# GpSimd's share of the products of delta u and B in a selective scan: one-tensor multiplies by a scalar of the partition, 20 of 64

## The chip, the cores and the metric

The kernel runs on one core of a Trainium2 chip. The metric is the device time of one execution in microseconds (us), as the median of the runs. A trace comes from one more execution, taken by the hardware profiler.

The engines are named as in the profile: PE is TensorE's matmuls and PEld its weight loads, DVE is VectorE, ACT is ScalarE, POOL is GpSimd, SP is SyncE. L1580 is line 1580 of the kernel.

## The reference, cut to what matters

Four layers follow one another on an image of 2 x 128 x 128 pixels with 128 channels: window attention, a Fourier layer, a recurrent convolution, and a selective scan over four orders of the pixels. Only the selective scan is touched. For each direction k it computes, over a sequence of L pixels, with 256 channels d and 16 states n:

```python
delta = softplus(delta + delta_bias)
def step(h, inp):
    ut, dt, bt, ct = inp
    dA = jnp.exp(dt[..., None] * A4)
    h = dA * h + (dt * ut)[..., None] * bt[:, :, None, :]
    y = jnp.einsum('bkdn,bkn->bkd', h, ct)
    return (h, y)
```

The term `(dt * ut)[..., None] * bt` is the product that the change is about: for each pixel, 256 channels of delta u times 16 values of B.

## The kernel before, in words

`layer3_scan` (L1245 onwards) cuts the work into 256 **parts**: 2 images x 4 directions x 32 stretches of 512 pixels. A part has 8 **slots**. Slot s holds 4 tiles of 128 rows (4 states x 32 channels) by 512 pixels; with `q, e = divmod(s, 2)`, q is the group of four states and e the half of the channels. All slots of all parts are numbered on, 2048 in all, and the loop at L1649 walks through them with a fixed lead or lag for each step:

- `exponentials(g + 1)` (L1554): four ACT instructions write `da`, the decay of each pixel (L1561), one slot ahead.
- `kept(g - 1)` (L1631): one small ACT copy saves the last state of the slot before (L1637). It waits for that slot's scans.
- `products(g + 2)` (L1566): the products of delta u and B, two slots ahead, into a buffer `but` (five of them). Here the rows are 128 pixels, and `bt[:, tb, c]` holds one value of B for each pixel. A slot makes 2 blocks of pixels (`j`) x 4 states (`n`) = 8 products of 128 x 256, so a part makes 64. Slot `2q` makes pixel blocks tb = 0 and 1 of the state group q, slot `2q + 1` makes tb = 2 and 3. Some go to POOL (L1580), the others to ACT (L1585).
- `weighted(g - 1)` (L1639): one POOL multiply of 128 x 2048 by C, in place (L1643).
- `tiles(g)` (L1604): for each of the four tiles PE turns four blocks of `but` into a PSUM tile `ups` (L1617, three buffers), and DVE runs the recurrence over it (L1625). A tile needs all four pixel blocks, so both slots of `products` of its state group.
- `sums(g - 2)` (L1589): PE sums the weighted states into `yps` (L1599).

In between, steps of the parts to come and of those done are placed by a written table (L1534): `projected` (ACT, L1358) at the head of slot 7, `softplus_a` (ACT, L1392 and L1393) at the head of slot 1, `softplus_c` (ACT, L1405) in the middle of slot 2, and some small DVE work among the scans (L1399, L1413, L1420, L1429, L1466, L1488, L1493).

`in_order` (L114) ties each engine to the order in which the program was written. So each engine runs its instructions one after the other as the loop emits them, and an engine that waits holds back everything that it has behind.

The buffers around the change are `but` (five), `hs` and `da` (three each), `du` and `bt` (two each). POOL issues no DMA in this stage, and SP's queue carries the loads and stores.

Before the change, POOL takes state `n == 3`, except pixel block 3 in the even groups q. That is 2 of a slot's 8 products in slots 0, 2, 3, 4, 6 and 7, and 1 in slots 1 and 5: 14 in a part. ACT makes the other 50.

Of the kernel before, what the change touches and what calls it, by code (L numbers as in the profile page):

```python
# [11 lines left out]
ALU = mybir.AluOpType  # L12
# [3 lines left out]
P = 128  # L16
# [1228 lines left out]
def layer3_scan(tc, cs, ins, xs, xst, yc, ys):  # L1245
# [11 lines left out]
    nc = tc.nc  # L1257
    NS, DR, NX, T = 16, 8, 40, 512
    with ExitStack() as ctx:
# [52 lines left out]
        def tag_of(i):  # L1312
            return "_".join(map(str, parts[i]))
# [252 lines left out]
        def products(g):  # L1566

            i, s = divmod(g, 8)
            q, half = divmod(s, 2)
            v = held[i]  # L1570
            but = five.tile([P, 2, 8, 4, 32], F32, name=f"but_{tag_of(i)}_{s}", tag="but")
            v[("but", q, half)] = but
            bt = v["bt"]
            du = v["du"].rearrange("p t (g c) -> p t g c", c=32)
            for j in range(2):
                tb = 2 * half + j
                for n in range(4):
                    c = DR + 4 * q + n
                    if n == 3 and (tb < 3 or q % 2):
                        nc.gpsimd.tensor_tensor(  # L1580
                            but[:, j, :, n, :], du[:, tb],
                            bt[:, tb, c : c + 1].unsqueeze(2).to_broadcast([P, 8, 32]), ALU.mult,
                        )
                    else:
                        nc.scalar.activation(  # L1585
                            but[:, j, :, n, :], du[:, tb], AF.Copy, scale=bt[:, tb, c : c + 1]
                        )
# [60 lines left out]
        with in_order(tc):  # L1648
            for g in range(-15, slots + 7):  # L1649
                at(g, "head")  # L1650
                if 0 <= g + 1 < slots:
                    exponentials(g + 1)
                if 0 <= g - 1 < slots:
                    kept(g - 1)
                at(g, "mid")
                if 0 <= g + 2 < slots:
                    products(g + 2)
                if 0 <= g - 1 < slots:
                    weighted(g - 1)
                if 0 <= g < slots:  # L1660
                    tiles(g)
                else:
                    for j in range(4):
                        at(g, j)
                if 0 <= g - 2 < slots:
                    sums(g - 2)
                at(g, "end")
# [230 lines left out]
```

## Time and profile before

| | us |
|---|---|
| runs shown: median of 3 (lowest to highest) | 18375.93 (18361.79 to 18383.79) |
| profiled execution, first to last instruction (span) | 18336.7 |
| DVE busy | 15970.0 (87%) |
| ACT busy | 14905.8 (81%) |
| PE busy | 14346.5 (78%) |
| POOL busy | 11817.0 (64%) |

The profiled execution has only its span in the records; the median of the runs is 39.2 us above that span. The shares in the table are means over four layers that differ much. The line of 40 slices, each 1/40 of the span, shows where the engines are busy (a digit is the busy share in tenths):

```profile
DVE  6776666336999899999999999999999999999996
ACT  4665666334546799999999999999999999999984
POOL 0000000011000599999999999999999999999981
```

POOL's digits rise to 9 in the 15th slice, at about 14/40 x 18337 = 6418 us, and stay there up to the 39th. This is the scan stage. Everything ahead of it (three layers and the convolution of the fourth) and the short stage behind it are not touched.

### The profile page before, as it was taken

To read this page: it belongs to the slowest core of one execution; us is meant where nothing else is said; L and a number is where in the kernel's file an instruction comes from. 1 tells how busy PE (TensorE), PEld (TensorE's weight loads), DVE (VectorE), ACT (ScalarE), POOL (GpSimd) and SP (SyncE) were. 2 spreads that over 40 slices of the span, in tenths; PEclk is the share of its full clock that TensorE was granted. 3 is DMA by queue.
4 is the path that set the end of the run, shared out by engine and by line. 5 is a ranking of instruction groups with operands and counts; after the bars stand their busy time and mean duration, and the time that the engine had idled before them with its cause. 6 is when DMAs were issued, how large, how long until landed. Compare 5 with 4: busy or idle time off the path is not lost. (4 is left out here: it accounts for less than half of the span.)

```text
span 18336.7 us, 277675 instructions
## 1 busy us (share of the span) xinstructions
PE 14346.5 (78%) x97794; PEld 8284.5 (45%) x97794; DVE 15970.0 (87%) x20729; ACT 14905.8 (81%) x30049; POOL 11817.0 (64%) x6490
## 2 busy tenths in 40 slices
PE   7888888887668677777777777777777777777778
PEld 5555555664223344444444444444444444444445
DVE  6776666336999899999999999999999999999996
ACT  4665666334546799999999999999999999999984
POOL 0000000011000599999999999999999999999981
PEclk9999999889889899999999999999999999999989
DMA  2000000121115544444444455544444444445546
GB/s 45 23 24 23 17 18 16 61 65 56 56 51 191 155 116 116 121 127 127 125 116 116 118 127 129 128 121 115 116 125 128 129 125 117 116 119 127 127 131 192
DMA packets 1232638, 1859.32 MB, mean 101 GB/s; under 512 B 124877, under 2 KB 591565, under 8 KB 1228942
## 3 DMA queue, kind: packets, MB, share of 16 engines
q1 hardware_dynamic: 1157374, 1817.40, 37.6%
q10 hardware_dynamic: 73872, 24.16, 0.5%
q8 instruction: 776, 12.71, 0.3%
q14 instruction: 616, 5.05, 0.1%
HBM read 1396.64 MB, written 444.60 MB: 100 GB/s over the span
## 5 line engine op out<-in xcount | busy, mean ns | idle before, releaser
L1625 DVE TENSOR_TENSOR_SCAN hs<-da,states,ups 128x512 f32<-128x512 f32 x8192 | 9931.7, 1265 | 255.4 <-PE ups L1617 238.7
L1643 POOL TENSOR_TENSOR hs<-hs,cb 128x2048 f32<-128x2048 f32 x2048 | 9399.9, 4590 | 318.0 <-POOL but L1580 198.6
L1617 PE MATMUL ups<-ident,but 128*128 128x128 f32 x32768 | 5560.5, 301 | 2617.4 <-DVE hs L1625 1715.1
L1617 PEld LDWEIGHTS ups<-ident,but 128*128 128x128 f32 x32768 | 3859.2, 150 | 6207.6 <-DVE hs L1625 3515.8
L1585 ACT ACTIVATE but<-du,bt 128x256 f32<-128x256 f32 x12800 | 5350.7, 500 | 4.5 <-DVE du L1466 4.2
L1561 ACT ACTIVATE da<-db,na 128x512 f32<-128x512 f32 x8192 | 5238.6, 713 | 18.6 <-DMA db<-dd 15.8
L1599 PE MATMUL yps<-hs,sel 128*32 128x512 f32 x16384 | 2482.5, 682 | 50.4 <-POOL hs L1643 44.3
L1580 POOL TENSOR_TENSOR but<-du,bt 128x256 f32<-128x256 f32 x3584 | 2148.5, 619 | 17.0 <-DVE du L1466 17.0
L306 POOL TENSOR_TENSOR xres<-xres,rowb 128x256 f32<-128x256 f32 x128 | 94.3, 737 | 2440.3 <-DMA xres<-in_x 1744.7
L391 ACT COPY pT<-tps 128x512 f32<-128x512 f32 x1280 | 723.6, 585 | 1104.3 <-PE tps L386 1104.1
L386 PE MATMUL tps<-ident,s 128*128 128x128 f32 x8192 | 1223.7, 286 | 437.4 <-DVE pT L389 271.0
L358 DVE CUSTOM_DVE_ANT_1 s<-sps,relbias 128x512 f32<-128x512 f32 x2048 | 1321.7, 683 | 133.2 <-PE sps L341 127.9
L386 PEld LDWEIGHTS tps<-ident,s 128*128 128x128 f32 x8192 | 896.4, 143 | 1029.4 <-issue 498.5
L371 ACT ACTIVATE s<-s,nm 128x1024 f32<-128x1024 f32 x1024 | 1166.2, 1141 | 126.8 <-DVE nm L369 124.1
L1156 POOL MEMSET xpad<- 128x34 f32 x8 | 1.3, 162 | 1170.1 <-PE xs L1030 1105.8
L341 PE MATMUL sps<-kc,qT 32*128 32x512 f32 x4096 | 614.7, 668 | 1.9 <-DVE qT L326 1.2
L1637 ACT COPY states<-hs 128x4 f32<-128x4 f32 x2048 | 384.4, 188 | 247.5 <-DVE hs L1625 247.5
L389 DVE COPY pT<-tps 128x512 f32<-128x512 f32 x768 | 528.1, 688 | 55.9 <-PE tps L386 53.2
L1599 PEld LDWEIGHTS yps<-hs,sel 128*32 128x32 f32 x16384 | 339.4, 114 | 476.1 <-issue 301.9
L1349 PE MATMUL xdps<-xc,xpw 128*40 128x512 f32 x1024 | 540.8, 610 | 12.4 <-POOL xd L1286 12.4
L734 POOL TENSOR_TENSOR xr<-xr,row_ln_b 128x512 f32<-128x512 f32 x64 | 81.2, 1271 | 708.2 <-DMA xr<-x 474.7
L1381 PE MATMUL dtps<-xd,dtw 65*128 65x512 f32 x1024 | 534.0, 603 | 0.0
(287 smaller groups left out, 16171.3 us busy)
## 6 DMA issues: line engine op xcount, KB each, us to landing
db<-dd SPq DMA_DIRECT2D x1024, 512.0 KB
cb<-cd SPq DMA_DIRECT2D x1024, 256.0 KB
xc<-xs SPq DMA_DIRECT2D x256, 512.0 KB
dd<-dl SPq DMA_DIRECT2D x256, 512.0 KB
ut<-xst SPq DMA_DIRECT2D x128, 512.0 KB
yc<-ysb SPq DMA_DIRECT2D x128, 512.0 KB
yf<-yc SPq DMA_DIRECT2D x128, 512.0 KB
ys<-yt SPq DMA_DIRECT2D x128, 512.0 KB
```

What stands on the lines that cost most here:

```text
L341: nc.tensor.matmul(sps, v["qT"][hp, qt * P : (qt + 1) * P], kc[b, wh + g][hp, ww : ww + 2].rearrange("p a r c -> p (a r c)"), start=True, ...
L358: nc.vector.tensor_tensor_reduce(blocks(v["s", qt][:, h, 512 * g : 512 * g + 512]), blocks(v["sps", qt, g][h]), bias[:, h, :, r0 : r0 + WS ...
L371: nc.scalar.activation(s[:, h, :], s[:, h, :], AF.Exp, bias=nm[:, 2, h : h + 1], scale=-1.0, accum_out=v["sums"][:, qt, h : h + 1],)
L386: nc.tensor.transpose(tps[:, j, :], v["s", qt][:, h, k0 : k0 + P], cs.ident)
L391: nc.scalar.copy(dst, tps)
L1561: nc.scalar.activation(da[:, j, :], held[i]["db"][:, 4 * e + j, :], AF.Exp, scale=na[:, k, c : c + 1])
L1580: nc.gpsimd.tensor_tensor(but[:, j, :, n, :], du[:, tb], bt[:, tb, c : c + 1].unsqueeze(2).to_broadcast([P, 8, 32]), ALU.mult,)
L1585: nc.scalar.activation(but[:, j, :, n, :], du[:, tb], AF.Copy, scale=bt[:, tb, c : c + 1])
L1599: nc.tensor.matmul(v["yps"][e][32 * j : 32 * j + 32, :], sel, hs[:, j, :], start=(q == 0), stop=(q == 3),)
L1617: nc.tensor.transpose(ups[:, tb * P : (tb + 1) * P], v[("but", q, tb // 2)][:, tb % 2, 4 * e + j].rearrange("p n c -> p (n c)"), cs.ident,)
L1625: nc.vector.tensor_tensor_scan(o, a, u, state[:, c0 + j : c0 + j + 1], ALU.mult, ALU.add)
L1643: nc.gpsimd.tensor_tensor(hs, hs, v["cb"][:, s // 2, :].unsqueeze(1).to_broadcast([P, 4, T]), ALU.mult)
```

## The change

In `products`, POOL's instruction is another one, and the choice of products is another one. The multiply by B was a `tensor_tensor` with two tensors, the second being one column of B, repeated 256 times by its access pattern. It becomes a `tensor_scalar`, with the same column as a scalar of each partition. POOL now takes state 3 of every pixel block, and state 2 of pixel block 3.

```diff
                 for n in range(4):
                     c = DR + 4 * q + n
-                    if n == 3 and (tb < 3 or q % 2):
-                        nc.gpsimd.tensor_tensor(
-                            but[:, j, :, n, :], du[:, tb],
-                            bt[:, tb, c : c + 1].unsqueeze(2).to_broadcast([P, 8, 32]), ALU.mult,
+                    if n == 3 or (n == 2 and tb == 3):
+                        nc.gpsimd.tensor_scalar(
+                            but[:, j, :, n, :], du[:, tb], bt[:, tb, c : c + 1], None, ALU.mult
                         )
                     else:
                         nc.scalar.activation(
```

Products of each engine in a slot, before and after:

| slot | POOL before | POOL after | ACT before | ACT after |
|---|---|---|---|---|
| 0, 2, 4, 6 | 2 | 2 | 6 | 6 |
| 1, 5 | 1 | 3 | 7 | 5 |
| 3, 7 | 2 | 3 | 6 | 5 |
| part | 14 | 20 | 50 | 44 |

## The prediction

> **What bounds the kernel now.** I read the slices first (only the scan stage holds POOL's products), then the busy times in windows inside that stage, then the groups of instructions, then the timelines of single engines over one part.
>
> The windows; columns are the window, its length, and each engine's busy us with its number of instructions:
>
> ```profile
> 9000.00:11000.00 2000.00, 1533.13 (x9405) 821.89 (x9398) 1964.79 (x1934) 1951.96 (x4198) 1952.41 (x967) 0.93 0.49 120
> 11000.00:13000.00 2000.00, 1550.42 (x9485) 836.88 (x9483) 1956.19 (x1927) 1955.47 (x4208) 1947.62 (x966) 0.92 0.48 123
> ```
>
> Three engines are full at once. Over the four windows from 9000 to 17000 us DVE is busy 7843.7 us of 8000 (98.0%), ACT 7827.2 (97.8%), POOL 7806.4 (97.6%); PE is at 77%. The stretch from 8000 to 17000 us holds 6317 scans, 32 of them to a part, so 197.4 parts of 45.6 us. **Per part: DVE 44.7 us busy, ACT 44.6, POOL 44.5**, each with 0.9 to 1.1 us idle.
>
> ```profile
> L1625 DVE TENSOR_TENSOR_SCAN hs<-da,states,ups 128x512 f32<-128x512 f32 x8192 | 9931.7, 1265 | 255.4 <-PE ups L1617 238.7
> L1643 POOL TENSOR_TENSOR hs<-hs,cb 128x2048 f32<-128x2048 f32 x2048 | 9399.9, 4590 | 318.0 <-POOL but L1580 198.6
> L1585 ACT ACTIVATE but<-du,bt 128x256 f32<-128x256 f32 x12800 | 5350.7, 500 | 4.5 <-DVE du L1466 4.2
> L1580 POOL TENSOR_TENSOR but<-du,bt 128x256 f32<-128x256 f32 x3584 | 2148.5, 619 | 17.0 <-DVE du L1466 17.0
> ```
>
> DVE has the most work, and its idle time stands almost wholly before the scan, waiting for PE's turned products (255.4 us over 256 parts, 1.0 us a part). The next question is what PE waits for then. First DVE, then PE, then ACT, over the same part:
>
> ```profile
> 10021.80 1.28 DVE L1625 TENSOR_TENSOR_SCAN hs<-da,states,ups 128x512 f32<-128x512 f32 x1 [0.29 <-PE ups L1617]
> 10028.76 1.28 DVE L1625 TENSOR_TENSOR_SCAN hs<-da,states,ups 128x512 f32<-128x512 f32 x1 [0.68 <-PE ups L1617]
> ```
>
> ```profile
> 10016.20 0.33 PE L1617 MATMUL ups<-ident,but 128*128 128x128 f32 x1 [0.70 <-ACT but L1585]
> 10027.07 0.35 PE L1617 MATMUL ups<-ident,but 128*128 128x128 f32 x1 [1.73 <-ACT but L1585]
> 10028.27 3.01 PE L1617 MATMUL ups<-ident,but 128*128 128x128 f32 x13 [0.85 <-ACT but L1585]
> ```
>
> ```profile
> 10007.49 0.20 ACT L1637 COPY states<-hs 128x4 f32<-128x4 f32 x1 [0.53 <-DVE hs L1625]
> 10013.23 2.91 ACT L1585 ACTIVATE but<-du,bt 128x256 f32<-128x256 f32 x7
> 10025.61 2.51 ACT L1585 ACTIVATE but<-du,bt 128x256 f32<-128x256 f32 x6
> ```
>
> DVE's two gaps are at the first scans of slots 1 and 2. Both lead to ACT's products. Those of slot 1 (the seven, done at 10016.05) hold back slot 0's first tile by 0.70, and PE, which then has the projections of the next part among slot 0's tiles, carries this into slot 1. Those of slot 3 (done at 10028.03) hold back slot 2's first tile, whose scan starts 0.73 us later. ACT itself last waited at 10007.49, for slot 5's scans; from there it runs without a pause and is late because the softplus falls into slot 1. So the last wait is ACT's, and the bound under it is DVE's 44.7.
>
> **The change: ACT's side.** Six ACT products go. A run of 6 takes 2.51 and one of 7 takes 2.91, so one is worth 0.40 us and a part 2.4 us of 44.6. Where they go matters: slot 1 loses two, slot 3 one. At 10016.05 ACT would be 0.8 us earlier, more than the 0.70 that PE waits. At 10028.03 it would be 1.2 us earlier, more than the 0.68 that DVE waits. Does a tile wait in between shift to `kept`? The saved states of slots 6, 7 and 0 were complete about 1.1, 1.8 and 4.0 us before their copies in a part that I followed slot by slot, so 0.8 us fits. As DVE closes its own gaps, the need comes earlier too: from slot 5's last scan to slot 2's first DVE takes 21.4 us with about 1.0 of gaps, so 20.4 without; ACT's chain takes 20.5 from that scan to the last product of slot 3, less 1.2, plus 0.73 to the scan: 20.1. It fits with 0.3 us. I therefore let DVE's 0.9 us a part go, but for 0.1: **44.8 us a part**, if POOL keeps up.
>
> **The change: POOL's side.** What a product costs POOL is read from start to start:
>
> ```profile
> 10001.78 1.18 POOL L1580 TENSOR_TENSOR but<-du,bt 128x256 f32<-128x256 f32 x2
> 10002.92 4.55 POOL L1643 TENSOR_TENSOR hs<-hs,cb 128x2048 f32<-128x2048 f32 x1
> 10007.43 1.18 POOL L1580 TENSOR_TENSOR but<-du,bt 128x256 f32<-128x256 f32 x2
> ```
>
> Two products take 1.14 us, 0.57 each, and 14 of them 8.0 us. The weighting takes 4.51 for eight times the elements: (4.51 - 0.57)/1792 = 2.2 ns an element for two inputs, with next to no fixed part.
>
> The after needs X, the price of a one-tensor multiply of 256 with a scalar of the partition. No row has it. The rows near it are copies, which read one tensor, and a `tensor_scalar` of 4 elements with an immediate:
>
> ```profile
> 75.08 0.21 POOL L251 COPY xp<-xp 128x16 f32<-128x16 f32 x1 [0.17 <-DVE xp L246]
> 75.23 0.28 POOL L252 COPY xp<-xp 128x112 f32<-128x112 f32 x1
> 75.46 0.21 POOL L253 COPY xp<-xp 128x16 f32<-128x16 f32 x1
> 145.55 0.53 POOL L416 COPY recx<-rec 128x128 f32<-128x128 f32 x2 [50.07 <-DVE rec L413]
> ```
>
> ```profile
> L416 POOL COPY recx<-rec 128x128 f32<-128x128 f32 x256 | 67.6, 294 | 586.1 <-DVE rec L413 586.1
> L51 POOL TENSOR_SCALAR rs<-mv 128x4 f32<-128x4 f32 x128 | 29.3, 229 | 618.3 <-DVE mv L1737 415.6 <-DVE mv L726 202.8
> ```
>
> From start to start a copy of 16 takes 0.15 and one of 112 takes 0.23: 0.8 ns an element and 0.14 fixed. At 256 that is 0.35. The `tensor_scalar` row, standing alone, is 0.03 above what a copy of 4 would take alone (0.212 less 12 x 0.8 ns = 0.20), which makes 0.37. **Lower end** 0.24: a copy's slope of 0.21 and as little fixed part as the first memsets show, which start 0.03 apart. **Upper end** 0.73: two inputs' slope (0.56) and the fixed 0.17, as if the scalar were read again for each element. I take **0.37**, by the rows that read one tensor, and 20 x 0.37 = 7.4 us: POOL falls from 44.5 to 43.9 and stays below DVE.
>
> As a formula: a part on POOL is 44.5 - 8.0 + 20 X, plus some 0.15 of idle where POOL paces the loop (it now idles 1.1 us, at slot 3, where it has caught up with the scans). So 36.65 + 20 X: it meets 44.8 at X = 0.41, and today's 45.6 at **X = 0.45**. Each 0.01 us of X past 0.41 costs 0.2 us a part, 51 us in all. Three products in a row, up to 1.7 us even at the old price, stand ahead of the weighting on POOL in slots' turns; behind them wait the weighting, PE's sums and then PE's next tiles. In the part that I followed, POOL's products of slot 3 ended 3.2 us before ACT's, so this order hides them. No DMA and no queue is moved.
>
> The Trainium skill (GPSIMD Engine Reference, 4.1 Engine selection) calls one-input work on GpSimd roughly line-rate, and the copies' 0.8 ns an element agree. But the same page (3.1 Elementwise) gives about 1.8 cycles an element as the best case of a tight loop, with 512 elements in 769 ns, and its section 7 charges some 102 cycles for a read command that doesn't overlap, which the scalar could be. By these an estimate of X is 0.38 alone, 0.47 with the extra read, and the copy's fixed part would bring it past 0.5: that speaks against the change, and the sum would be 46 to 47 us a part. No run here shows either.
>
> **Sum.** 0.8 us x 256 parts = 205 us off the span of 18336.7, so 18132. The runs' median stands 39 us above that span, which gives **18170**.
>
> **Rivals.**
> - *GpSimd's `tensor_scalar` is no cheap form.* Place: POOL, which then paces the loop; it decides from X = 0.45 on. For it: three engines are level, so POOL has only 1.1 us a part to give, and the L51 row says little of the slope. Against: the copies. At X = 0.50 a part takes 46.65, and the time is 18376 + 256 x 1.05 = 18645; at the old 0.57 it takes 48.05 and gives 19003; at 0.73 it takes 51.25 and gives 19822. DVE would wait for PE, PE for POOL's weighting.
> - *ACT gets its relief and POOL takes it back*: X of 0.44 to 0.45, between 36.65 + 8.8 = 45.45 and today's 45.6. Within 0.2% of before: about 18360.
> - *The gaps go only in part*: PE is the next to be late. In slot 0 it turns four tiles, does the next part's projections and the sums before slot 1's first tile, and that gap of about 0.3 us stays while slot 2's goes. Then 0.5 us a part: 18376 - 128 = 18248. For it: the wait for ACT there is only 0.70, two slots' work before the gap. Against: the order on PE is fixed, so what starts 0.7 earlier should end earlier.
>
> **How the numbers follow.** DVE paces, gaps gone: 0.36. Gaps gone in part, or POOL slightly above DVE (X 0.41 to 0.44): 0.16. POOL gives it back: 0.05. POOL paces above today's time: 0.43, since X's bounds put 0.45 inside the upper part of the range 0.24 to 0.73 and the scalar's fetch is unseen. So faster 0.52, same 0.05, slower 0.43; 0.2% (37 us) is about what a measurement of this kernel can tell from no change. The likeliest case's own range is 18130 (DVE's busy 44.7 with no idle at all gives 18145, and a little less POOL traffic could help DVE) to 18300. The whole range goes from 18120 to 18990, which holds X up to the old price; beyond it lies 0.1, below it almost nothing.
>
> **What would show it.** The mean of the new POOL row from start to start (0.37 against 0.45 and more); POOL's busy share in the windows (98% of a shorter part, or 99.5%); DVE's idle before the scan (255 us down to some 30, or up with POOL at the end of the wait); ACT's idle before `kept` up by the 2.4 us a part that it no longer works, less what the part gets shorter. The prediction is wrong if X is above 0.45, or if the scans themselves get slower or quicker beside the new form.

## The result, and the profile after

The changed kernel takes 20692.24 us (median of 4 runs, 20664.83 to 20698.52), the kernel before 18379.86 us beside it: the ratio is 1.1258 (95% interval 1.1242 to 1.1274). That is 9.0 us more for each of the 256 parts, and outside the range of the prediction.

The groups of the profile after, from its page (line numbers past 1580 are one lower than before):

```profile
L1624 DVE TENSOR_TENSOR_SCAN hs<-da,states,ups 128x512 f32<-128x512 f32 x8192 | 10078.8, 1265 | 2022.4 <-PE ups L1616 1568.8
L1642 POOL TENSOR_TENSOR hs<-hs,cb 128x2048 f32<-128x2048 f32 x2048 | 9302.8, 4542 | 63.3 <-ACT states L1636 63.2
...
L1580 POOL TENSOR_SCALAR but<-du,bt 128x256 f32<-128x256 f32 x5120 | 4784.9, 951 | 17.1 <-DVE du L1466 17.1
L1584 ACT ACTIVATE but<-du,bt 128x256 f32<-128x256 f32 x11264 | 4711.7, 496 | 5.7 <-DVE du L1466 4.2
...
L1636 ACT COPY states<-hs 128x4 f32<-128x4 f32 x2048 | 390.7, 191 | 1803.4 <-DVE hs L1624 1800.8
...
L1399 DVE TENSOR_SCALAR up<-ae 128x1024 f32<-128x1024 f32 x256 | 595.8, 2327 | 5.1 <-ACT ae L1393 5.1
```

GpSimd's product now takes 951 ns, where the tensor_tensor took 619 and the prediction had put 0.37 us from start to start. VectorE's idle time before the scan is 2022 us, up from 255, so the gaps that were to go have grown eightfold. ScalarE waits 1803 us for the scans.

The windows of the profile after (window, length, then busy time and instructions of PE, PEld, DVE, ACT, POOL; granted clock; DMA share; GB/s):

```profile
9000.00:11000.00 2000.00, 1441.61 (x7872) 769.19 (x7870) 1708.37 (x1611) 1560.06 (x3284) 1996.26 (x1026) 0.82 0.40 100
11000.00:13000.00 2000.00, 1443.36 (x7971) 773.43 (x7968) 1718.10 (x1608) 1569.58 (x3306) 1992.82 (x1023) 0.83 0.42 105
```

GpSimd is busy 99.7% of the time, VectorE 86%, ScalarE 78%. One engine is full instead of three. The waits of the changed kernel from 8000 to 18000 us (engine and tile, whom it waited for, us in all, times, longest) say how this reaches the others:

```profile
PE yps L1598 <- POOL hs L1642: 1634.5, 1154, 2.5
ACT states L1636 <- DVE hs L1624: 1260.8, 752, 7.5
DVE hs L1624 <- PE ups L1616: 1118.3, 763, 3.0
```

PE's sums wait for GpSimd's weighting, and all that PE has behind them, the next tiles too, waits with them; VectorE waits for PE's tiles; ScalarE's copies of the states wait for VectorE. GpSimd's own timeline has no pause left:

```profile
10006.27 3.18 POOL L1580 TENSOR_SCALAR but<-du,bt 128x256 f32<-128x256 f32 x3
10009.41 4.54 POOL L1642 TENSOR_TENSOR hs<-hs,cb 128x2048 f32<-128x2048 f32 x1
10013.94 1.81 POOL L1580 TENSOR_SCALAR but<-du,bt 128x256 f32<-128x256 f32 x2
10015.73 4.52 POOL L1642 TENSOR_TENSOR hs<-hs,cb 128x2048 f32<-128x2048 f32 x1
10020.24 2.71 POOL L1580 TENSOR_SCALAR but<-du,bt 128x256 f32<-128x256 f32 x3
10022.92 4.54 POOL L1642 TENSOR_TENSOR hs<-hs,cb 128x2048 f32<-128x2048 f32 x1
```

Three products take 2.68 us from the start of the run of three to the start of the weighting behind it (10020.24 to 10022.92), two take 1.79: **0.89 to 0.90 us each**. The first run of three, at 10006.27, took 3.14; an experiment below says why.

### The profile page after: what moved, and what is told of

It is laid out like the page before. It is cut to its first block, busy times and chain, and to the rows that moved or that the text cites. A ratio compares the mean times of both kernels' runs of the same rounds, so it can differ in the third digit from the quotient of the medians.

```text
span 20684.6 us, 277675 instructions
## 1 busy us (share of the span) xinstructions
PE 15452.3 (75%) x97794; PEld 8843.4 (43%) x97794; DVE 16524.6 (80%) x20729; ACT 14416.9 (70%) x28513; POOL 14392.7 (70%) x8026
## 5 line engine op out<-in xcount | busy, mean ns | idle before, releaser
L1624 DVE TENSOR_TENSOR_SCAN hs<-da,states,ups 128x512 f32<-128x512 f32 x8192 | 10078.8, 1265 | 2022.4 <-PE ups L1616 1568.8
L1642 POOL TENSOR_TENSOR hs<-hs,cb 128x2048 f32<-128x2048 f32 x2048 | 9302.8, 4542 | 63.3 <-ACT states L1636 63.2
L1616 PE MATMUL ups<-ident,but 128*128 128x128 f32 x32768 | 5926.0, 323 | 1635.3 <-DVE hs L1624 1327.0
L1616 PEld LDWEIGHTS ups<-ident,but 128*128 128x128 f32 x32768 | 4318.4, 163 | 5641.2 <-DVE hs L1624 2833.6
L1580 POOL TENSOR_SCALAR but<-du,bt 128x256 f32<-128x256 f32 x5120 | 4784.9, 951 | 17.1 <-DVE du L1466 17.1
L1584 ACT ACTIVATE but<-du,bt 128x256 f32<-128x256 f32 x11264 | 4711.7, 496 | 5.7 <-DVE du L1466 4.2
L1598 PE MATMUL yps<-hs,sel 128*32 128x512 f32 x16384 | 2977.7, 808 | 2277.2 <-POOL hs L1642 2274.3
L1392 ACT ACTIVATE ae<-dtps 128x512 f32<-128x512 f32 x512 | 305.2, 596 | 725.1 <-PE dtps L1381 723.5
L1381 PE MATMUL dtps<-xd,dtw 65*128 65x512 f32 x1024 | 628.3, 700 | 0.0
L1399 DVE TENSOR_SCALAR up<-ae 128x1024 f32<-128x1024 f32 x256 | 595.8, 2327 | 5.1 <-ACT ae L1393 5.1
```

The lines of the kernel that those rows point to most:

```text
L1381: nc.tensor.matmul(ps, dtw[:, k, e * P : (e + 1) * P], v["xd"], start=True, stop=True)
L1580: nc.gpsimd.tensor_scalar(but[:, j, :, n, :], du[:, tb], bt[:, tb, c : c + 1], None, ALU.mult)
L1584: nc.scalar.activation(but[:, j, :, n, :], du[:, tb], AF.Copy, scale=bt[:, tb, c : c + 1])
L1598: nc.tensor.matmul(v["yps"][e][32 * j : 32 * j + 32, :], sel, hs[:, j, :], start=(q == 0), stop=(q == 3),)
L1616: nc.tensor.transpose(ups[:, tb * P : (tb + 1) * P], v[("but", q, tb // 2)][:, tb % 2, 4 * e + j].rearrange("p n c -> p (n c)"), cs.ident,)
L1624: nc.vector.tensor_tensor_scan(o, a, u, state[:, c0 + j : c0 + j + 1], ALU.mult, ALU.add)
```

## The experiments

**1. The form alone, and the count alone.** `form14` keeps the selection of before and takes the new instruction; `count20` keeps the instruction and takes the new selection.

```diff
 form14
-                        nc.gpsimd.tensor_tensor(
-                            but[:, j, :, n, :], du[:, tb],
-                            bt[:, tb, c : c + 1].unsqueeze(2).to_broadcast([P, 8, 32]), ALU.mult,
+                        nc.gpsimd.tensor_scalar(
+                            but[:, j, :, n, :], du[:, tb], bt[:, tb, c : c + 1], None, ALU.mult
 count20
-                    if n == 3 and (tb < 3 or q % 2):
+                    if n == 3 or (n == 2 and tb == 3):
```

> Only the form of the instruction changes: the 14 products that GpSimd had before, as tensor_scalar. Theory (GpSimd paces the part, and one such product takes 0.90 us from start to start as in the profile after): a part is 44.5 - 8.0 + 14 x 0.90 + 0.15 = 49.25 us, and the time 18376 + 256 x 3.65 = 19310 us, with GpSimd at over 99% in the scan stage. Rival (the count of 20 is what overloads GpSimd, and the form costs little by itself): within 100 us of before, 18380. Second rival (the price rises with the number in a row or with GpSimd's lateness, not with the form): a product well below 0.90 us here.

> Only the count changes: 20 products on GpSimd, as tensor_tensor at 0.57 us each. Theory: a part is 36.65 + 20 x 0.572 = 48.1 us, and the time 18376 + 256 x 2.5 = 19015 us; GpSimd over 99% busy, ScalarE waiting for the scans. Rival (moving work off ScalarE gains what the prediction said, and GpSimd has hidden slack): 18170 to 18400. If form and count simply add on GpSimd, form14, count20 and the change itself lie on one line 36.5 us + count x price.

Measured, one run each beside 18369.49 for the kernel before: form14 19536.84 us, count20 19944.54 us. The form alone costs 1167 us, 4.6 us a part; 14 x (0.90 - 0.57) = 4.6. The expectation was 227 us lower, because it let GpSimd's idle time shrink to 0.15 us a part, and it stayed at about 1 us (busy 7838.75 us of 8000). The count alone missed by 930 us, though the product's row stood at 619 ns as before. GpSimd was only 92% busy (7346.65 of 8000), and VectorE 99.3% (7940.99). So count20 is a case of another kind. Its VectorE timeline:

```profile
10007.27 7.75 DVE L1399 TENSOR_SCALAR up<-ae 128x1024 f32<-128x1024 f32 x1
10014.94 1.27 DVE L1625 TENSOR_TENSOR_SCAN hs<-da,states,ups 128x512 f32<-128x512 f32 x1
```

and GpSimd's over the same stretch:

```profile
10002.61 4.53 POOL L1643 TENSOR_TENSOR hs<-hs,cb 128x2048 f32<-128x2048 f32 x1
10007.09 1.76 POOL L1580 TENSOR_TENSOR but<-du,bt 128x256 f32<-128x256 f32 x3
10008.80 4.53 POOL L1643 TENSOR_TENSOR hs<-hs,cb 128x2048 f32<-128x2048 f32 x1
10013.28 1.19 POOL L1580 TENSOR_TENSOR but<-du,bt 128x256 f32<-128x256 f32 x2
10016.58 4.54 POOL L1643 TENSOR_TENSOR hs<-hs,cb 128x2048 f32<-128x2048 f32 x1 [2.11 <-ACT states L1637]
```

L1399 adds 1 to 1024 elements of each partition. It took 7.75 us here; in the kernel before it took 0.67. It starts at 10007.27, while GpSimd is at work, and ends at about 10015.0, soon after GpSimd's products end at 14.47 and leave it idle for 2.11 us. One product of GpSimd was running when it started, five more instructions ran through from start to end in that time, and GpSimd did not stop between them. In the kernel before, the lines of VectorE, GpSimd and ScalarE at the same step:

```profile
10025.57 0.67 DVE L1399 TENSOR_SCALAR up<-ae 128x1024 f32<-128x1024 f32 x1
```

```profile
10023.82 1.18 POOL L1580 TENSOR_TENSOR but<-du,bt 128x256 f32<-128x256 f32 x2
10025.84 4.81 POOL L1643 TENSOR_TENSOR hs<-hs,cb 128x2048 f32<-128x2048 f32 x1 [0.84 <-POOL but L1580]
```

```profile
10025.53 0.18 ACT L1637 COPY states<-hs 128x4 f32<-128x4 f32 x1
```

L1399 starts at 10025.57, inside the pause of 0.84 us that GpSimd makes between 10025.00 and 10025.84. In 247 of the 256 parts it was so, with GpSimd's next start some 0.26 us after L1399's; in eight, L1399 met a running weighting and took 1.8 to 4.99 us. GpSimd's pause, in turn, exists because its weighting of slot 0 waits for ScalarE's copy of the states, and ScalarE is late in slot 1. The bracket names GpSimd's own product as the one waited for, but that had ended at 10025.00; the copy ended at 10025.71, 0.13 us before the weighting started, and 0.13 us is the median over all parts. The weighting of slot 0 then takes 4.81 us (median) where those of the other slots take 4.56, so L1399 seems to hold it up a little in turn.

The Trainium skill (SBUF - State Buffer, Who interferes with whom) states that VectorE and GpSimd share one pair of SBUF ports, that VectorE's tensor_scalar can run over both pairs, and that the shared pair is then locked for a whole instruction. The rows above agree, and go further: in count20 the wait lasted over several GpSimd instructions, and not only the one that was running.

**2. The lock by itself.** Four kernels, in one set with 18354.55 us for the kernel before. The first is the kernel before with L1399 placed one scan later. The second is count20 with the sum done by ScalarE, the third the change with the same edit. The fourth, `place14`, has the form and the count of before, and gives GpSimd more of slots 1 and 3, where ScalarE is late.

```diff
 up_one_scan_later
-            (-7, 0, turned_b), (-7, 2, softplus_b),
+            (-7, 0, turned_b), (-7, 3, softplus_b),
 count20_up_on_act, after_up_on_act
-            nc.vector.tensor_scalar(up, v["ae"], 1.0, None, ALU.add)
+            nc.scalar.activation(up, v["ae"], AF.Copy, bias=1.0)
 place14
-                    if n == 3 and (tb < 3 or q % 2):
+                    if n == 3 and (j == 0 or s < 5) or n == 2 and j == 1 and s == 3:
```

> The kernel before, with nothing changed but the place of L1399: after the fourth scan of slot 1 in place of after the third. Theory (port): it comes some 1.2 us later, when GpSimd has begun its weighting, waits for GpSimd's next idle time, and takes 4 to 8 us and not 0.67; a part is 3 to 6 us longer, 19100 to 19900 us. Rival (no such lock; the 7.6 us in count20 came with the load on GpSimd): within 100 us of before.

Measured: 19028.13 us, 674 us more than before for the same instructions in almost the same order. L1399's row (duration in ns: least, median, longest):

```profile
L1399 DVE TENSOR_SCALAR up<-ae x256: 671/4153/4171, 6126.7 to 18424.3; 128x1024 f32<-128x1024 f32 x128
```

The median is 4153 ns, where it was 670. In 255 of the 256 parts it now comes during a weighting, 0.93 us after its start, and ends 0.55 us past that weighting's end (medians). Here it got in at the next boundary of GpSimd's instructions, in count20 it did not; what decides this was not settled. So **L1399's 0.67 us in the kernel before depended on its place beside a pause of GpSimd**, and the lock makes it 3.5 us longer where it is met like this.

> count20 (20 tensor_tensor on GpSimd), and L1399's sum 1 + ae done by ScalarE (about 1.06 us a part by the row of L1393) and not by VectorE. Theory (port): GpSimd paces, 36.65 + 20 x 0.572 = 48.1 us a part, 19015 us, and VectorE's idle time before the scan comes back. Rival (VectorE is slowed by something else that L1399's row only shows): about 19900 us as in count20.

Measured: 18875.87 us, 1069 us less than count20. Its groups:

```profile
L1625 DVE TENSOR_TENSOR_SCAN hs<-da,states,ups 128x512 f32<-128x512 f32 x8192 | 9968.9, 1268 | 897.3 <-PE ups L1617 848.1
L1643 POOL TENSOR_TENSOR hs<-hs,cb 128x2048 f32<-128x2048 f32 x2048 | 9330.7, 4556 | 68.3 <-ACT states L1637 68.1
```

VectorE has idle time before the scan again (897 us), and GpSimd hardly any (68). A part takes 47.7 us (from the two spans: 18874.1 less 18336.7 is 537 us, 2.1 us a part more than 45.6), where the formula 36.65 + 20 x 0.572 gave 48.1. The formula holds within 0.5 us where L1399 is out of its way.

> The change, with L1399's sum done by ScalarE. Theory (GpSimd alone paces the changed kernel, 8 weightings of 4.51 and 20 products of 0.90, and L1399's longer row is hidden): 20600 to 20700 us, as the change. Rival (the port costs the changed kernel too): 20000 to 20500 us.

Measured: 20507.21 us, some 185 us below the change (0.7 us a part), between the two expectations. GpSimd was busy 8000.00 us of 8000. So L1399's use of the ports took a little from the changed kernel as well, and the timelines point to GpSimd's side: the run of three products that took 3.14 us and not 2.68, from 10006.27 on, met L1399, which ran from 10005.61 to 10006.85. More than nine tenths of the loss stay, with GpSimd never idle: that much is GpSimd's price.

> Form and count of before (14 tensor_tensor), but GpSimd takes them where ScalarE is late: 2 in slot 1 and 3 in slot 3, 1 in slots 5, 6 and 7. The prediction's theory (ScalarE's products of slots 1 and 3 are the last wait, VectorE is the bound below): VectorE's idle time of 1.0 us a part goes in part or wholly, 18170 to 18300 us. Rival found in count20 (VectorE's tensor_scalar L1399 runs through a port that it shares with GpSimd, and in the kernel before it happens to fall into GpSimd's one idle gap of 0.9 us a part, which is there because ScalarE is late): the gap moves or closes, L1399 goes from 0.67 us to 5 us or more, and the time is 19000 us or more.

Measured: 19116.26 us, ratio 1.0418 (1.0400 to 1.0435), as the rival had it. Groups of place14, and L1399's row in it:

```profile
L1625 DVE TENSOR_TENSOR_SCAN hs<-da,states,ups 128x512 f32<-128x512 f32 x8192 | 9933.1, 1264 | 196.3 <-PE ups L1617 174.7
L1643 POOL TENSOR_TENSOR hs<-hs,cb 128x2048 f32<-128x2048 f32 x2048 | 9369.6, 4575 | 1062.1 <-ACT states L1637 1058.5
```

```profile
L1399 DVE TENSOR_SCALAR up<-ae x256: 671/3510/6910, 6116.7 to 18482.4; 128x1024 f32<-128x1024 f32 x128
```

VectorE's idle time before slot 2's first scan went from 0.60 us a part (mean over all parts of the trace) to 0.002, which the prediction's step on ScalarE had forecast. But L1399's longer row stands just ahead of that gap and can fill it by itself: in up_one_scan_later, with ScalarE's products as before, it is 0.000 too. So place14 does not show that ScalarE's relief closed it. The smaller gaps in slots 0 and 1 did not go (0.38 before, 0.75 here). But L1399's median is 3510 ns, and up to 6910: its mean of 3.9 us costs more than all gaps together were worth.

**3. Where the 0.90 us come from.** `imm20` is the change with a constant as the scalar; it leaves the multiply by B out of GpSimd's 20 products. `probe` is the kernel before with rows of its own on GpSimd at the start, while GpSimd has nothing else to do.

```diff
 imm20
-                            but[:, j, :, n, :], du[:, tb], bt[:, tb, c : c + 1], None, ALU.mult
+                            but[:, j, :, n, :], du[:, tb], 0.5, None, ALU.mult
 probe (excerpt: one of each kind, at 256 elements; each is issued three times; pc is one column)
+                    nc.gpsimd.tensor_scalar(pb[:, 0:256], pa[:, 0:256], pc, None, ALU.mult)
+                    nc.gpsimd.tensor_scalar(
+                        po[:, :, 3, :], pa[:, 0:256].rearrange("p (g c) -> p g c", c=32), pc, None, ALU.mult
+                    )
+                    nc.gpsimd.tensor_scalar(pb[:, 0:256], pa[:, 0:256], 0.5, None, ALU.mult)
+                    nc.gpsimd.tensor_copy(pb[:, 0:256], pa[:, 0:256])
+                    nc.gpsimd.tensor_tensor(
+                        pb[:, 0:256], pa[:, 0:256], pc.to_broadcast([P, 256]), ALU.mult
+                    )
```

> As the change, but the scalar is the constant 0.5 in place of a column of B: GpSimd's 20 products of a part leave out the multiply by B. Theory A (the price is that of the tensor_scalar form itself, scalar or constant): 0.90 us a product and about 20690 us in all. Theory B (fetching the scalar of the partition from memory is what costs): a product of 0.57 us or less, and 19000 us or less; at 0.37 us 18170 to 18380.

> The kernel before, with rows added on GpSimd alone at the start, while it has nothing else to do: three each of tensor_scalar with a scalar of the partition (16, 256 and 1024 elements, and 256 with the strided output of the change), tensor_scalar with a constant (16, 256, 1024), copy (256, 1024) and tensor_tensor with a broadcast column (256, 1024). The starts of neighbours give slope and fixed part. Theory A (form): both tensor_scalar forms have a slope near 3 ns an element and little fixed part, 0.8 to 0.9 us at 256; copies 0.8 ns. Theory B (fetch): the constant is at a copy's slope, the scalar of the partition has the same slope and some 0.5 us more fixed part. Theory C (contention in the scan stage with VectorE's reads and writes): 256 elements take about 0.4 us here and 0.9 only in the scan. Theory D (stride): the strided output alone takes 0.9. The time of the whole is at most 60 us above before.

Measured: imm20 20370.83 us, with a product of 875 ns against 951; the probe 18382.88 us. GpSimd's timeline of the probe; each line is three instructions of one size, their start and the time of all three:

```profile
2.00 1.19 POOL L1799 TENSOR_SCALAR pb<-pa,pc 128x16 f32<-128x16 f32 x3
3.28 2.96 POOL L1801 TENSOR_SCALAR pb<-pa,pc 128x256 f32<-128x256 f32 x3
6.33 8.72 POOL L1803 TENSOR_SCALAR pb<-pa,pc 128x1024 f32<-128x1024 f32 x3
15.03 2.96 POOL L1805 TENSOR_SCALAR po<-pa,pc 128x256 f32<-128x256 f32 x3
18.06 0.93 POOL L1809 TENSOR_SCALAR pb<-pa 128x16 f32<-128x16 f32 x3
19.08 2.71 POOL L1811 TENSOR_SCALAR pb<-pa 128x256 f32<-128x256 f32 x3
21.87 8.48 POOL L1813 TENSOR_SCALAR pb<-pa 128x1024 f32<-128x1024 f32 x3
30.41 1.33 POOL L1815 COPY pb<-pa 128x256 f32<-128x256 f32 x3
31.80 3.25 POOL L1817 COPY pb<-pa 128x1024 f32<-128x1024 f32 x3
35.14 2.00 POOL L1819 TENSOR_TENSOR pb<-pa,pc 128x256 f32<-128x256 f32 x3
37.21 5.84 POOL L1823 TENSOR_TENSOR pb<-pa,pc 128x1024 f32<-128x1024 f32 x3
```

With a scalar of the partition (the lines that read `pa,pc`), three of 256 take 2.96 us, so a single one 0.93 with the pause between neighbours taken off; three of 1024 take 8.72. (8.72 - 2.96)/(3 x 768) = **2.50 ns an element**. The constant (the lines that read `pa` alone) has the same slope, (8.48 - 2.71)/2304 = 2.50, and some 0.08 us less fixed part. The strided output (L1805) costs exactly what the flat one does (L1801). The copy, which is also one tensor in and one out, has (3.25 - 1.33)/2304 = 0.83, and tensor_tensor with the broadcast column (5.84 - 2.00)/2304 = 1.67. So theory A holds: it is the form, in isolation as in the scan stage. The fetch of the scalar, worth 0.08 us, does not explain it, nor does the stride, nor VectorE beside it. An element costs half as much again in the form with one tensor input as in the form with two that it replaced.

**4. Is there a version that beats both?** Experiment 2 points to place14 with L1399 away from the shared ports. Three ways were tried, each with an own interval beside 18379.26 us.

```diff
 place14_up_two_inputs
+            nc.vector.scalar_tensor_tensor(up, v["ae"], 1.0, v["ae"], ALU.add, ALU.max)
 place14_up_accum
+            bl = one.tile([P, 1], F32, name=f"bl_{tag_of(i)}", tag="bl")
+            nc.vector.tensor_scalar(up, v["ae"], 1.0, 0.0, ALU.add, ALU.add, accum_out=bl)
 place15_up_on_act
+                    if n == 3 and (j == 0 or s < 6) or n == 2 and j == 1 and s == 3:
+            nc.scalar.activation(up, v["ae"], AF.Copy, bias=1.0)
```

> place14, with L1399's sum in a form of VectorE that streams its input twice (scalar_tensor_tensor: (ae + 1) max ae, the same value) and so can't run over both ports. Theory (port): no waits of several us; the row costs some 1.2 us in place of 0.67, VectorE 45.3 us a part, and with the gap of slot 2 gone some 45.4: 18300 to 18350 us. Rival (two inputs from SBUF contend with GpSimd as the port does): L1399 at 4 us or more again, 19000 us.

Measured: 19118.4 us, 1.0405 (1.0374 to 1.0436). The row of the sum:

```profile
L1399 DVE SCALAR_TENSOR_TENSOR up<-ae x256: 1192/3100/7498, 6132.0 to 18588.4; 128x1024 f32<-128x1024 f32 x128
```

Two inputs from SBUF met the same wait, 1192 ns at best and 7498 at worst: the rival.

> place14, with L1399 still a tensor_scalar of VectorE with one input, but with a second output that sums the row. If that form doesn't use the shared port, as the Trainium skill says (SBUF - State Buffer, Who interferes with whom), it takes about 1.1 us without waits, VectorE 45.2 us a part, 18280 to 18350 us; if it does, as place14: about 19100 us.

Measured: 18467.96 us, 1.0054 (1.0038 to 1.0071).

```profile
L1400 DVE TENSOR_SCALAR_CACHE_REDUCE up<-ae x256: 1181/1193/1219, 6120.3 to 17848.4; 128x1024 f32<-128x1024 f32 x128
```

The row never waits: 1181 to 1219 ns over 256 parts. This is what the Trainium skill (SBUF - State Buffer, Who interferes with whom) states of that form, and the two inputs of the run before are on its list of those that contend. The time is 650 us below place14, and 89 above the kernel before, so the hoped-for 18280 to 18350 was missed: the row costs 0.52 us a part more than L1399's 0.67, and of VectorE's idle time before the scans 250 us stay; by slot, nearly all of it is in slots 0 and 1.

> 15 tensor_tensor on GpSimd (2 in slots 0 to 2, 3 in slot 3, 2 in slots 4 and 5, 1 in 6 and 7), L1399's sum on ScalarE. Theory: VectorE falls to 44.1 us a part, GpSimd stands at 36.65 + 15 x 0.572 = 45.2, ScalarE at 44.6 + 1.0 - 0.4 = 45.2; so 45.2 to 45.6, 18270 to 18376 us. Rival (any load past 44.7 on two engines at once costs more through the order of the program): 18450 us or more.

Measured: 18382.04 us, 1.0001 (0.9992 to 1.0011), just above the first expectation. Its window:

```profile
9000.00:17000.00 8000.00, 6277.17 (x37757) 3352.78 (x37756) 7714.44 (x7529) 7871.55 (x16792) 7831.68 (x4026) 0.91 0.49 122
```

VectorE (third pair) is down from 98.0% to 96.4%, ScalarE up from 97.8% to 98.4%, GpSimd from 97.6% to 97.9%: what VectorE was relieved of, the other two took on. None of the three beats the kernel before.

## Why the prediction was wrong

**The step that failed is the price X.** It was put at 0.37 us, with an upper end of 0.73; it is 0.90. The prediction argued from the rows that read one tensor, copies above all, and carried their slope of 0.8 ns an element over to an arithmetic form. The probe shows 2.50, three times that. The upper end failed for the same reason: it took the two-input rows' 2.2 ns as the worst that a one-input form could do. The only row of the same operation (L51, 229 ns at 4 elements) could have warned that it held nothing on the slope; the prediction said so for the rival and yet left 0.73 as the end. The 2.2 ns were themselves read from two kinds of row, the weighting with two full tensors and the product with a repeated column; in the probe the latter alone has 1.67 ns an element and a fixed part of some 0.19 us, not next to none.

**The formula was right.** 36.65 + 20 x 0.90 = 54.65 us a part; the scan stage took 54.69 (13999.6 us from the first scan to the last, over 256). Some of this closeness is luck: without L1399 on the ports it took 54.0 (after_up_on_act: 13827.8 us from the first scan to the last). The rival "GpSimd's tensor_scalar is no cheap form" was the case, at a price beyond its list. Its chain of waits (VectorE for PE, PE for the weighting) is what the profile shows.

**GpSimd's idle time was misread.** The prediction put 1.1 us a part down to slot 3, where GpSimd had caught up with the scans. Most of it, 0.9 us, is the weighting of slot 0 waiting for ScalarE's late copy of the states. This is the pause in which L1399 fits. So the sum left a term out: relief for ScalarE closes the pause (the wait before the weighting of slot 0 goes from 0.90 us a part to 0.10 in place14, with 14 products as before), and L1399 then waits for the ports. At X = 0.57 the prediction's figure was 19003; count20 took 19944.54.

**ScalarE's side stays open.** Since GpSimd paced the changed kernel, none of it could show there. The gap of slot 2 is gone in place14 (0.60 to 0.002 us a part) and in place14_up_accum (0.000), but VectorE comes to it later in both: its row just ahead is longer, by 3.2 us in the mean and by 0.52, and the gaps of slots 0 and 1 grew. What ScalarE's relief closes by itself was not told apart. The gaps of slots 0 and 1 went from 0.38 us to 0.75 in place14, and L1399's stall does not keep them there: place14_up_accum, where that row never waits, has 0.97. For slot 0's first scan ScalarE is still the last there: in the median part the scan starts 0.48 us after ScalarE's last product for it, the least distance in the trace. A possible reason, not tested, is that place14 gives ScalarE one product more in each of slots 6 and 7, just ahead of these. Whether ScalarE or PE's own order makes the gap of slot 1 was not told apart.

**The two rules from the Trainium skill.** "Roughly line-rate" for one input (GPSIMD Engine Reference, 4.1 Engine selection) fits the copies (0.83 ns an element in the probe) and not tensor_scalar (2.50). The estimate that spoke against the change, from 1.8 cycles an element (the same page, 3.1 Elementwise) with an extra read (its section 7), came out past 0.5 us with a copy's fixed part: the right side of 0.45, and still well below the 0.90 measured.

## What to carry to other kernels

Price an instruction on GpSimd by a row of the same operation at two sizes; where there is none, let the bound reach past the neighbours, since one tensor less to read can still cost more. Where three engines are level, ask of each short idle gap what else uses it: here a pause of 0.9 us, itself a sign of ScalarE's lateness, let a VectorE instruction of 0.67 us through that takes up to 7.9 us where the gap is gone (count20).

## What the runs showed of the hardware that was not expected

VectorE's tensor_scalar of 128 x 1024 waited up to 7.9 us over several GpSimd instructions that followed one another without a pause (count20, median 7900 ns). In place14 both cases stand in one run: in 101 of the 256 parts it got in at the next boundary of GpSimd's instructions (0.67 to 1.12 us), in 120 it took 6.3 to 6.9 us. In the changed kernel it comes near the end of a weighting and gets in there, at a median of 1420 ns; the product behind is then longer. What decides where it finds room was not tried.

PE's instructions got longer on average in the changed kernel: the sums (128 x 512) went from 682 ns before to 808 after, the turns from 301 to 323, at a granted clock of 0.92 and 0.82 in the scan stage. The medians stayed at 617 and 273 ns: more of them took the longer time that some took before (1.06 us for a sum). PE is not what sets the end there.
